# Four-image vision tower on one core: the last image's turn in another order, the block list in five steps, and the expert weights fetched expert by expert into the keys' tile

## The chip, the core and the metric

The program runs on one core of a Trainium2 chip. The metric is the device time of one execution in microseconds. Before the change three executions took 757.95, 759.25 and 761.08 us; the median is 759.25 us.

## The reference

Four images of 3 x 224 x 224 are cut into patches of 8 x 8, which makes 784 tokens of 256 channels for each image. A tokenizer is followed by two layers. The part that matters here is layer 0:

```python
h = tok(x)                                        # [4, 3*784, 256]; the three copies of 784 rows are equal
mn = layernorm(layernorm(h)) * gamma + beta
q, k, v = mn @ Wq, mn @ Wk, mn @ Wv               # 8 heads of 32 channels
g = sigmoid(mn @ Wg + bg)
att = einsum('slhc,tlhc->sth', q, k) * scale      # image s against image t, summed over the tokens
att = softmax(att, axis=1)
h = h + (einsum('sth,tlhc->slhc', att, v) * g).reshape(4, -1, 256) @ Wo + bo
x = layernorm(h)
lg = softmax(relu(x @ router_w1 + b1) @ router_w2 + b2)    # 6 experts
top_w, top_i = top_k(lg, 2)
w = softmax(top_w)
y_e = relu(relu(x @ W1[e]) @ W2[e]) @ W3[e]       # each expert, with biases
h = h + w[0] * y_{top_i[0]} + w[1] * y_{top_i[1]}
```

Attention is between images, with one share for each head and pair of images. Each row then goes through two of six experts. Layer 1 (linear attention and a second mixture of experts) follows and isn't touched.

## The kernel before, in words

**Layout.** All is f32. The residual `h` lies in 25 tiles of 128 rows: six for each image, and a last one with the 16 rows left over of each image. Queries, keys, values and gates are kept turned, with channels on the partitions and the image's 784 tokens along the free axis, in two halves `o` of 128 channels. Keys and queries share one tile, `kq` (L767): first the keys `kT` of half 0 (four images), then of half 1, then two slots for the queries of the current and of the next image.

**Layer 0, image by image.** Four functions make up an image `s`: `products` (L815; a multiplication of the image's queries with the keys of image `t`, with a sum along the tokens, on DVE), `shares_before` and `shares_after` (L827, L841; the matmul `pl` with a head mask, then a softmax of 8 numbers for each partition), `gate_mm` and `gate_act` (L799, L808; matmuls `pg`, then a tanh on ACT), and `first_value` and `values` (L856, L865; the weighted sum of the four images' values, then the gate). `attended` (L883) multiplies by `Wo` (`pwo`), adds to `h` on DVE (L897), negates the mean `nm` (L901) and sums squares on ACT (L903). `scales_of`, `shifts_of` and `rows_of_part` (L909, L914, L920) normalise the rows for the experts; `turn_part`, `router`, `router_logits` (L939, L953, L963) turn them and compute the router's logits; `choose` (L975) takes the two best of six on DVE; `count` (L1027) ranks the rows within their experts with matmuls (`pcount`); `send` (L1043) writes the positions, and GpSimd scatters the rows with indirect DMAs (L1059), 12 for an image, into `xrows` in DRAM, sorted by expert.

**Block list.** `early_blocks` (L1109) is a generator of three steps. It counts the rows of each expert so far (`ptotal`, L1079), marks full blocks of 256 rows (`full`, L1114), numbers them (`pplace`, L1087, and a copy, L1089) and writes for the first seven blocks the row offset and the expert's offset into an integer tile `meta` (`pmeta`, L1097; L1101).

**Experts.** For each block, `load` (L1369) reads the row offset into a register of SyncE (SP) and fetches 256 rows (`xb`); `own_weights` (L1391) reads the expert's offset into a register of DVE and copies that expert's 1540 columns out of the tile `ew` (L1396); `turned` (L1398) turns the rows (`ptb`) and copies them on ACT; `hidden` (L1411) runs two layers (`pb`); `rows_back` (L1431) runs the third (`pyb`), adds the bias and stores to `yrows`. A `load` of an early block waits for the scatters of images 0 and 1 alone, any later one for all.

**What sets the order.** PE, ACT and DVE follow the order written by hand inside `tc.manual_schedule`; SP does so where the block names it. The last image's turn starts at L1455: first the remaining `products`, with the gates, `send` of image 1's rows and the block list between them; then the attention's pool is closed (L1477), a new tile `ew` is taken from the pool of `kq` (L1479), and six DMAs of 768 KB on SP fetch the weights of all experts (L1486 to L1491), with four loads of blocks behind them. As `ew` takes the place of `kq`, the six DMAs wait for the last reader of `kq`. Four loads of layer 1's weights stand next on SP. Then come the values of image 3, the rest of image 2's routing, image 3's attention in the parts `ua` (tiles 0 to 3) and `ub` (4 to 6), and, woven in, the first blocks.

Of the kernel before, what the change touches and what calls it, by code (L numbers as in the profile page):

```python
# [21 lines left out]
F32 = mybir.dt.float32  # L22
I32 = mybir.dt.int32
# [4 lines left out]
P = 128  # L28
TT = 128
NI = 4  # L30
# [9 lines left out]
D = 256  # L40
# [9 lines left out]
E0 = 6  # L50
# [7 lines left out]
NEARLY = -(-(2 * 2 * TPI * TT - E0 * (BLK - 1)) // BLK)  # L58
# [4 lines left out]
EW = 6 * D + 4  # L63
# [5 lines left out]
def tile_vit_tower(ctx: ExitStack, tc: tile.TileContext, a: dict, out: bass.AP):  # L69
    nc = tc.nc  # L70
# [694 lines left out]

    keys = layer0.enter_context(tc.tile_pool(name="keys", bufs=1, reuse_waits="tile"))
    kq = keys.tile([P, 2 * TOK + 4 * SEQ], F32, tag="kq", name="kq")  # L767
    kT = kq[:, : 2 * TOK].rearrange("p (c n) -> p c n", c=2)
    qT2 = kq[:, 2 * TOK :].rearrange("p (s c n) -> p s c n", s=2, c=2)
    att = ctx.enter_context(ExitStack())  # L770
# [44 lines left out]
    def products(s, o, ts=range(NI)):  # L815
        if s >= NI:
            return
        if s not in atts:
            atts[s] = small.tile([P, 2, NI], F32, tag="part", name="part")
        for t in ts:  # L820
            prod = attm.tile([P, SEQ], F32, tag="prod", name="prod")
            nc.vector.scalar_tensor_tensor(  # L822
                prod, qTs[s][:, o, :], 1.0, kT[:, o, t * SEQ : (t + 1) * SEQ],
                ALU.mult, ALU.mult, accum_out=atts[s][:, o, t : t + 1],
            )
# [258 lines left out]
    def numbered(these):  # L1084

        pp = psum_s.tile([P, 512], F32, tag="pss", name="pplace")[:NQ, :1]
        nc.tensor.matmul(pp, before[:NQ, :NQ], these, start=True, stop=True)  # L1087
        place = small.tile([NQ, 1], F32, tag="place", name="place", bufs=1)
        nc.vector.tensor_copy(place, pp)  # L1089
        return place  # L1090

    def meta_of(these, place, n):
        here = small.tile([NQ, NBLK], F32, tag="here", name="here", bufs=1)[:, :n]
        nc.vector.tensor_scalar(here, blk[:, :n], place, these, ALU.is_equal, ALU.mult)
        pm = psum_s.tile([P, 512], F32, tag="pss", name="pmeta")
        for k in range(3):
            nc.tensor.matmul(  # L1097
                pm[:1, k * n : (k + 1) * n], tcol[:, k + 1 : k + 2], here, start=True, stop=True
            )
        meta = small.tile([1, 3, n], I32, tag=f"meta{n}", name="meta", bufs=1)  # L1100
        nc.vector.tensor_tensor(  # L1101
            meta, pm[:1, : 3 * n].rearrange("r (k i) -> r k i", k=3), shift[:, :, :n], ALU.add
        )
        return meta

    metas = {}
    taken = small.tile([NQ, 1], F32, tag="taken", name="taken", bufs=1)

    def early_blocks():  # L1109

        pn = rows_in_all()
        yield
        full = small.tile([NQ, 1], F32, tag="full", name="full", bufs=1)
        nc.vector.scalar_tensor_tensor(  # L1114
            full, pn, -float(BLK), tcol[:, 0:1], ALU.add, ALU.is_ge
        )
        place = numbered(full)
        yield
        nc.vector.tensor_scalar(taken, place, float(NEARLY), full, ALU.is_lt, ALU.mult)
        metas[0] = meta_of(full, place, NEARLY)  # L1120
        yield

    def flag(name, n=1):
# [151 lines left out]
    )  # L1275
    junk = route.tile([TT, D], F32, tag="junk", name="junk")

    def added_rows(s):

        roots_next()  # L1280
        past = (s - 2, 0, TPI)
        if s > 1:
            products(s, 0, [NI - 1])
            choose(past)
        for k, two in enumerate(halves(range(TPI))):
            if s == 1:
                products(s, 0, (range(2), [2], [3])[k])
            elif k == 2:
                products(s, 1, [0])
            attended(s - 1, two)  # L1290
        if s > 1:
            count(past)
# [36 lines left out]
        if s > 1:  # L1329
            mix3(past)  # L1330

    with tc.manual_schedule(engines=by_hand):
        for o in range(2):
            products(0, o, [NI - 1])
        weights_of_images(0)
        gate_mm(0, 0)
        gate_mm(0, 1)
        gate_act(0, 0)
        first_value(0, 0, 0, SEQ, nc.vector)
        first_value(0, 1, 0, SEQ, nc.scalar)  # L1340
        gate_act(0, 1)
        values(0, 0, 0, SEQ)
        for o in range(2):
            q_mm(1, o)
            q_copy(1, o)
        values(0, 1, 0, SEQ)
        keep_left(0)
        for s in range(1, NI - 1):
            added_rows(s)
            weighed(s)  # L1350
        added_rows(NI - 1)
# [103 lines left out]
    s = NI - 1  # L1455
    past, u, ua, ub = (s - 2, 0, TPI), (s - 1, 0, TPI), (s, 0, GT), (s, GT, TPI + 1 - GT)
    rest = (GN, SEQ - GN)
    with tc.manual_schedule(engines=by_hand):
        products(s, 1, [1])
        scales_of(u)  # L1460
        send(past)
        steps = early_blocks()
        next(steps)
        gate_mm(s, 0)
        shifts_of(u)
        products(s, 1, [2])
        next(steps)
        products(s, 1, [3])
        next(steps)
        gate_act(s, 0)  # L1470
        mx = shares_before(s)
        gate_mm(s, 1)
        for _ in steps:
            pass
        gate_act(s, 1)
        shares_after(s, mx)
    att.close()  # L1477
    work[0] = layer0.enter_context(tc.tile_pool(name="blocks", bufs=2, reuse_waits="tile"))
    ew = keys.tile([P, E0, EW], F32, tag="kq", name="ew")  # L1479
    ewf[0] = ew.rearrange("p e n -> p (e n)")  # L1480
    eb3 = work[0].tile([P, E0 * D], F32, tag="eb3", name="eb3", bufs=1)
    nc.gpsimd.dma_start(
        out=eb3, in_=a["L0_ffn_expert_b3"].rearrange("e n -> (e n)").partition_broadcast(P)
    )
    with tc.manual_schedule(engines=by_hand | {ENG.SP}):
        for i, name in enumerate(("expert_w1", "expert_w2", "expert_w3")):  # L1486
            for c in range(2):
                nc.sync.dma_start(
                    out=ew[:, :, (2 * i + c) * D : (2 * i + c + 1) * D],
                    in_=a[f"L0_ffn_{name}"].rearrange("e (c p) n -> c p e n", p=P)[c],  # L1490
                )  # L1491
        for i in range(4):
            load(i)
        first_value(s, 0, 0, GN, nc.vector)
        first_value(s, 1, 0, GN, nc.scalar)
        rows_of_part(u)
        mix1(past)
        values(s, 0, 0, GN)
        values(s, 1, 0, GN)
        turn_part(u)  # L1500
        mix2(past)
        for o in range(2):
            first_value(s, o, *rest, nc.scalar)
        values(s, 0, *rest, range(1, 3))
        attended(s, [0, 1])
        values(s, 0, *rest, range(3, NI))
        attended(s, [2, 3])
        mix3(past)
        values(s, 1, *rest)
        keep_left(s)  # L1510
        router(u)
        scales_of(ua)
        router_logits(u)
        attended(s, [4, 5])
        shifts_of(ua)
        rows_of_part(ua)
        attended(s, [6])
        for i in (0, 1):
            b = cols[:, rows[f"eb{i + 1}_0"] :][:, : 2 * E0].rearrange("p (e r) -> p e r", r=2)
            nc.vector.tensor_copy(ew[:, :, 6 * D + 2 * i : 6 * D + 2 * i + 2], b)  # L1520
        choose(u)
        turned(0)
        turn_part(ua)
        own_weights(0)
        scales_of(ub)
        count(u)
        hidden(0, 0)
        shifts_of(ub)
        rows_of_part(ub, both=True)
        own_weights(1)  # L1530
        turned(1)
        router(ua)
        send(u)
        hidden(0, 1)
        turn_part(ub, both=True)
        router_logits(ua)
        own_weights(2)
        hidden(1, 0)
        rows_back(0)
        load(4)  # L1540
        choose(ua)
        router(ub)
        turned(2)
        hidden(1, 1)
        count(ua)
        hidden(2, 0)
        send(ua)
        rows_back(1)
        load(5)
        router_logits(ub)  # L1550
        own_weights(3)
        turned(3)
        hidden(2, 1)
        choose(ub)
        hidden(3, 0)
        rows_back(2)
        load(6)
        own_weights(4)
        count(ub)
        turned(4)  # L1560
        hidden(3, 1)
        send(ub)
        hidden(4, 0)
        rows_back(3)
        own_weights(5)
        turned(5)
        steps = later_blocks()
        hidden(4, 1)
        next(steps)
        hidden(5, 0)  # L1570
        next(steps)
        rows_back(4)
        next(steps)
        load(7)
        load(8)
        own_weights(6)
        turned(6)
        hidden(5, 1)
        next(steps)
        hidden(6, 0)  # L1580
        next(steps)
        rows_back(5)
        load(9)
        for v in (u, ua, ub):
            mix1(v)
        hidden(6, 1)
        for v in (u, ua, ub):
            mix2(v)
        for v in (u, ua, ub):
            mix3(v)  # L1590
# [715 lines left out]
```

## Time and profile before

| What | Value |
|---|---|
| profiled execution | 760.57 us |
| its span, first to last instruction | 758.9 us |
| median of three executions | 759.25 us |
| PE (matmul) busy | 698.0 us, 92% |
| DVE busy | 480.9 us, 63% |
| ACT busy | 331.1 us, 44% |
| mean granted TensorE clock | 0.975 |
| last image's turn, 241 to 293 us: PE busy | 40.9 of 52 us, granted clock 0.80 |
| expert blocks, 293 to 408 us: PE busy | 106.6 of 115 us, granted clock 1.00 |

The last two rows are the profile's busy times of stretches of the span. A stretch in which one engine is busy nearly throughout is bound by it; one in which none is holds waits between engines, and then the timeline (each instruction with the idle time before it and what ended that) is the view to read. PE records come in pairs, [...]so `gate_mm`'s four products are eight records. A PE record is longer where the granted clock is half.

### The profile page before, as it was taken

To read this page: it belongs to the slowest core of one execution; us is meant where nothing else is said; L and a number is where in the kernel's file an instruction comes from. 1 tells how busy PE (TensorE), PEld (TensorE's weight loads), DVE (VectorE), ACT (ScalarE), POOL (GpSimd) and SP (SyncE) were. 2 spreads that over 40 slices of the span, in tenths; PEclk is the share of its full clock that TensorE was granted. 3 is DMA by queue.
4 is the path that set the end of the run, shared out by engine and by line. 5 is a ranking of instruction groups with operands and counts; after the bars stand their busy time and mean duration, and the time that the engine had idled before them with its cause. 6 is when DMAs were issued, how large, how long until landed. Compare 5 with 4: busy or idle time off the path is not lost.

```text
span 758.9 us, 10590 instructions
## 1 busy us (share of the span) xinstructions
PE 698.0 (92%) x3391; PEld 478.9 (63%) x3391; DVE 480.9 (63%) x1521; ACT 331.1 (44%) x782; POOL 127.1 (17%) x231
## 2 busy tenths in 40 slices
PE   6798989999996879998899999888999999999996
PEld 4645565666564568887788874557677765555553
DVE  4666786778999654456544767799957464444441
ACT  0554776555865554342222326353546322222231
POOL 5400000000034607600003036752000000000000
PEclk9999999999999879999999999899999999999998
DMA  8399999100011864422334352321000013222333
GB/s 196 89 426 424 425 424 424 48 1 1 0 36 48 275 239 136 157 83 78 91 98 125 98 161 71 88 79 43 1 0 2 4 29 114 93 76 62 125 108 98
DMA packets 56117, 96.24 MB, mean 127 GB/s; under 512 B 6375, under 2 KB 46030, under 8 KB 56062
## 3 DMA queue, kind: packets, MB, share of 16 engines
q1 hardware_dynamic: 49648, 79.38, 29.6%
q0 software_dynamic: 5536, 14.32, 6.2%
q10 hardware_dynamic: 878, 1.86, 1.0%
q8 instruction: 27, 0.44, 0.2%
q14 instruction: 28, 0.23, 0.1%
HBM read 30.45 MB, written 65.09 MB: 126 GB/s over the span
## 4 chain that ended last, share of the span: by engine, by line
PE 69%; DVE 19%; ACT 5%; DMA 3%; issue 2%; SPq 1%; DVEq 1%; ACTq 0%
PE pb L1420 12%; PE pe L289 6%; PE pyb L1438 5%; PE ps L289 4%; PE pqk L1881 4%; PE pkv L289 4%; PE pt L280 4%; PE pw L558 3%; PE pwp L300 3%; PE ps L2256 3%; PE pout L2055 3%; PE pout L2060 3%; DVE oT L868 2%; PE pukx L1980 2%; DMA img<-in_x_dram 2%
## 5 line engine op out<-in xcount | busy, mean ns | idle before, releaser
L1059 POOL DMA_INDIRECT xrows<-xn,pos x50 | 52.6, 1051 | 238.0 <-DVE nm L918 191.9
L1643 POOL DMA_INDIRECT ys<-yrows,pos x50 | 51.7, 1033 | 142.7 <-DMA yrows<-yb 124.3
L1420 PE MATMUL pb<-xTb,own 128*128 128x256 f32 (+1 forms) x240 | 54.5, 371 | 8.1 <-DVE own L1396 5.4
L1426 ACT ACTIVATE hb<-pb,own 128x256 f32<-128x256 f32 (+1 forms) x74 | 33.8, 456 | 57.8 <-PE pb L1420 51.5
L1420 PE MATMUL pb<-hb,own 128*128 128x256 f32 (+1 forms) x240 | 52.1, 359 | 0.6 <-DVE hb L1428 0.6
L1438 PE MATMUL pyb<-own,hb 128*128 128x256 f32 x216 | 51.8, 381 | 0.2 <-ACT hb L1426 0.2
L1420 PEld LDWEIGHTS pb<-xTb,own 128*128 128x128 f32 x240 | 41.7, 195 | 16.1 <-ACT hb L1426 7.6
L1881 PE MATMUL pqk<-Wqkv,lxT 128*128 128x512 f32 x100 | 46.6, 613 | 0.2 <-ACT lxT L89 0.2
L289 PE MATMUL pe<-xT,eW 128*128 128x512 f32 (+1 forms) x112 | 46.0, 553 | 0.0
L1438 PEld LDWEIGHTS pyb<-own,hb 128*128 128x128 f32 x216 | 40.3, 190 | 5.9 <-ACT hb L1426 0.6
L1420 PEld LDWEIGHTS pb<-hb,own 128*128 128x128 f32 x240 | 40.5, 190 | 5.3 <-DVE hb L1428 1.2
L558 PE MATMUL pw<-Wall,pT 128*128 128x512 f32 x96 | 42.6, 593 | 0.0
L1409 ACT COPY xTb<-ptb 128x512 f32<-128x512 f32 (+1 forms) x30 | 16.2, 540 | 56.4 <-PE ptb L1405 56.4
L1444 DVE TENSOR_TENSOR yb<-pyb,eb 128x512 f32<-128x512 f32 (+1 forms) x30 | 19.1, 638 | 33.9 <-PE pyb L1438 33.5
L280 PE MATMUL pt<-ident,xn 128*128 128x128 f32 x200 | 30.4, 282 | 10.2 <-DVE xn L584 6.6
L280 PEld LDWEIGHTS pt<-ident,xn 128*128 128x128 f32 x200 | 23.5, 142 | 25.2 <-ACT y L561 6.0
L1428 DVE TENSOR_SCALAR hb<-pb,own 128x256 f32<-128x256 f32 (+1 forms) x46 | 20.5, 447 | 27.9 <-PE pb L1420 21.2
L822 DVE SCALAR_TENSOR_TENSOR prod<-kq 128x784 f32<-128x784 f32 x32 | 30.4, 970 | 6.1 <-ACT kq L1236 3.4
L289 PEld LDWEIGHTS pe<-xT,eW 128*128 128x128 f32 x112 | 20.2, 190 | 21.6 <-issue 16.5
L1396 DVE COPY own<-ew 128x1540 f32 x30 | 28.9, 965 | 6.8 <-ACT xTb L1409 2.7
L1895 ACT ACTIVATE qk<-qk 128x256 f32<-128x256 f32 x50 | 20.4, 408 | 28.4 <-DVE qk L1887 26.0
L1881 PEld LDWEIGHTS pqk<-Wqkv,lxT 128*128 128x128 f32 x100 | 19.0, 197 | 20.4 <-issue 17.9
(416 smaller groups left out, 1473.4 us busy)
## 6 DMA issues: line engine op xcount, KB each, us to landing
xrows<-nothing SPq DMA_DIRECT2D x22, 896.0 KB
yrows<-nothing SPq DMA_DIRECT2D x22, 896.0 KB
out_dram<-h SPq DMA_DIRECT2D x23, 384.0 KB
xb<-xrows SPq DMA_DIRECT2D x24, 256.0 KB
yrows<-yb SPq DMA_DIRECT2D x24, 256.0 KB
ew<-in_L_ffn_expert_w_dram SPq DMA_DIRECT2D x6, 768.0 KB
wb<-wd SPq DMA_DIRECT2D x16, 128.0 KB
img<-in_x_dram SPq DMA_DIRECT2D x2, 588.0 KB
```

The source lines that it names most:

```text
L280: nc.tensor.transpose(pt[:, j * TT : (j + 1) * TT], xn[:, j, c * P : (c + 1) * P], ident[:TT, :TT])
L289: nc.tensor.matmul(pm[: wcols.stop - wcols.start, :n], w[:, c, wcols], xT(c), start=(c == 0), stop=(c == chunks - 1),)
L300: nc.tensor.matmul(pm[:, i, :], xT(c, t), w[:, c, :], start=(c == 0), stop=(c == chunks - 1))
L558: nc.tensor.matmul(pm, pixels(c, tiles[j]), Wall[:, c, :], start=(c == 0), stop=(c == 1))
L822: nc.vector.scalar_tensor_tensor(prod, qTs[s][:, o, :], 1.0, kT[:, o, t * SEQ : (t + 1) * SEQ], ALU.mult, ALU.mult, accum_out=atts[s][:, o ...
L1059: put = nc.gpsimd.indirect_dma_start(out=xrows[:, :], out_offset=bass.IndirectOffsetOnAxis(ap=pos[:, k, t0 + j : t0 + j + 1], axis=0), in_ ...
L1396: nc.vector.tensor_copy(w, ewf[0][:, bass.ds(off, EW)])
L1420: nc.tensor.matmul(pm, wm[:, c, o * P : (o + 1) * P], src[:, c, :], start=(c == 0), stop=(c == 1),)
L1426: nc.scalar.activation(dst[:, o, :], pm, AF.Relu, bias=b)
L1438: nc.tensor.matmul(pm[:, t, :], src[:, c, t * P : (t + 1) * P], wm[:, c, :], start=(c == 0), stop=(c == 1),)
L1643: got = nc.gpsimd.indirect_dma_start(out=y[:, j, k, :], out_offset=None, in_=yrows[:, :], in_offset=bass.IndirectOffsetOnAxis(ap=pos[:, k, ...
L1881: nc.tensor.matmul(pqk, xTs[u][:, c, cut(j, 1)], Wqkv[:, c, : 2 * D], start=(c == 0), stop=(c == 1),)
```

## The change

Four things change, all around the last image's turn; no arithmetic changes.

- The weights' tile `ew` becomes a view of `kq`, without a new allocation. The six DMAs become 18 of 256 KB, three for each expert, so that each waits only for the readers of the region that it overwrites. Those of experts 0 and 1 are issued after the last product with half 0 of the keys, that of expert 2 after product (half 1, image 1), the rest after product (half 1, image 3).
- The block list has five steps: the matmul and the copy of `numbered`, and the matmuls and the sum of `meta_of`, are apart. All four `gate_mm` products of the image come before it, so that on PE the order is `pcount`, all of `pg`, `ptotal`, `pplace`, `pl`, `pmeta`; product (half 1, image 3) comes ahead of the copy of `pplace` on DVE, and `taken`, `here` and `meta` go between the steps of the softmax and the values. On ACT both gates come ahead of the first value of half 1.
- The four first `load`s come after the values of half 0 in program order; on SP they still follow all weights.
- `router(u)` comes before `attended(s, [0, 1])`; `own_weights(0)` and `own_weights(1)` come ahead of `choose(u)`, the first one ahead of `attended(s, [4, 5])`'s DVE part; `turned(0)` is ahead of `attended(s, [6])`; `hidden(0, 0)` ahead of `turn_part(ua)`; `count(u)` behind `router(ua)`.

```diff
+    ew = kq[:, : E0 * EW].rearrange("p (e n) -> p e n", e=E0)
...
-        place = numbered(full)
+        pp = psum_s.tile([P, 512], F32, tag="pss", name="pplace")[:NQ, :1]
+        nc.tensor.matmul(pp, before[:NQ, :NQ], full, start=True, stop=True)
+        yield
+        place = small.tile([NQ, 1], F32, tag="place", name="place", bufs=1)
+        nc.vector.tensor_copy(place, pp)
         yield
         nc.vector.tensor_scalar(taken, place, float(NEARLY), full, ALU.is_lt, ALU.mult)
-        metas[0] = meta_of(full, place, NEARLY)
+        pm, meta = meta_mm(full, place, NEARLY)
+        yield
+        metas[0] = meta_out(pm, meta, NEARLY)
         yield
...
+    def expert_weights(es):
+        for e in es:
+            for i, name in enumerate(("expert_w1", "expert_w2", "expert_w3")):
+                nc.sync.dma_start(
+                    out=ew[:, e, 2 * i * D : 2 * (i + 1) * D].rearrange("p (c n) -> p c n", c=2),
+                    in_=a[f"L0_ffn_{name}"][e].rearrange("(c p) n -> p c n", p=P),
+                )
...
             products(s, 0, [NI - 1])
+            if s == NI - 1:
+                expert_weights(range(2))
             choose(past)
...
-    with tc.manual_schedule(engines=by_hand):
+    with tc.manual_schedule(engines=by_hand | {ENG.SP}):
+        gate_mm(s, 0)
+        gate_mm(s, 1)
         products(s, 1, [1])
+        expert_weights([2])
         scales_of(u)
         send(past)
         steps = early_blocks()
         next(steps)
-        gate_mm(s, 0)
         shifts_of(u)
         products(s, 1, [2])
         next(steps)
+        gate_act(s, 0)
         products(s, 1, [3])
+        expert_weights(range(3, E0))
         next(steps)
-        gate_act(s, 0)
         mx = shares_before(s)
-        gate_mm(s, 1)
-        for _ in steps:
-            pass
+        next(steps)
         gate_act(s, 1)
         shares_after(s, mx)
     att.close()
...
-    ew = keys.tile([P, E0, EW], F32, tag="kq", name="ew")
-    ewf[0] = ew.rearrange("p e n -> p (e n)")
+    ewf[0] = kq[:, : E0 * EW]
...
-        for i, name in enumerate(("expert_w1", "expert_w2", "expert_w3")):
-            for c in range(2):
-                nc.sync.dma_start(
-                    out=ew[:, :, (2 * i + c) * D : (2 * i + c + 1) * D],
-                    in_=a[f"L0_ffn_{name}"].rearrange("e (c p) n -> c p e n", p=P)[c],
-                )
-        for i in range(4):
-            load(i)
...
         values(s, 0, 0, GN)
+        for _ in steps:
+            pass
+        for i in range(4):
+            load(i)
         values(s, 1, 0, GN)
...
             first_value(s, o, *rest, nc.scalar)
+        router(u)
         values(s, 0, *rest, range(1, 3))
         attended(s, [0, 1])
         values(s, 0, *rest, range(3, NI))
         attended(s, [2, 3])
         mix3(past)
+        scales_of(ua)
         values(s, 1, *rest)
         keep_left(s)
-        router(u)
-        scales_of(ua)
         router_logits(u)
-        attended(s, [4, 5])
         shifts_of(ua)
-        rows_of_part(ua)
-        attended(s, [6])
...
+        own_weights(0)
+        attended(s, [4, 5])
+        rows_of_part(ua)
+        turned(0)
+        attended(s, [6])
+        hidden(0, 0)
+        turn_part(ua)
+        own_weights(1)
+        scales_of(ub)
         choose(u)
-        turned(0)
-        turn_part(ua)
-        own_weights(0)
-        scales_of(ub)
-        count(u)
-        hidden(0, 0)
+        turned(1)
         shifts_of(ub)
         rows_of_part(ub, both=True)
-        own_weights(1)
-        turned(1)
         router(ua)
+        count(u)
         send(u)
```

More of the change, by code (lines that the diff above doesn't have):

```diff
@@ L1090, in numbered, with meta_mm @@
         return place
-    def meta_of(these, place, n):
+    def meta_mm(these, place, n):
         here = small.tile([NQ, NBLK], F32, tag="here", name="here", bufs=1)[:, :n]
@@ L1099, in meta_of, with meta_out @@
             )
-        meta = small.tile([1, 3, n], I32, tag=f"meta{n}", name="meta", bufs=1)
+        return pm, small.tile([1, 3, n], I32, tag=f"meta{n}", name="meta", bufs=1)
+    def meta_out(pm, meta, n):
         nc.vector.tensor_tensor(
@@ L1104, in meta_of @@
         return meta
+    def meta_of(these, place, n):
+        return meta_out(*meta_mm(these, place, n), n)
     metas = {}
@@ L1457, in tile_vit_tower @@
     rest = (GN, SEQ - GN)
-    with tc.manual_schedule(engines=by_hand):
+    with tc.manual_schedule(engines=by_hand | {ENG.SP}):
+        gate_mm(s, 0)
+        gate_mm(s, 1)
         products(s, 1, [1])
+        expert_weights([2])
         scales_of(u)
```

## The prediction

> **What bounds the kernel now.** I read the slices first, then busy times by stretch, then the timeline of the weak stretch, then SP's waits.
>
> ```profile
> PE   6798989999996879998899999888999999999996
> ...
> PEclk9999999999999879999999999899999999999998
> DMA  8399999100011864422334352321000013222333
> ```
>
> PE is nearly full everywhere except at the start and in slices 13 to 15 (digits 6, 8, 7; a slice is 19 us), where the clock also drops and the DMA engines are busy. That is the last image's turn.
>
> ```profile
> 200.00:241.00 41.00, 36.08 (x164) 25.65 (x162) 37.96 (x117) 26.47 (x60) 13.68 (x12) 1.00 0.11 39
> 241.00:293.00 52.00, 40.91 (x161) 29.38 (x162) 29.78 (x106) 28.92 (x70) 19.53 (x20) 0.80 0.59 203
> 293.00:408.00 115.00, 106.61 (x591) 91.74 (x590) 60.48 (x154) 37.02 (x84) 20.27 (x25) 1.00 0.33 106
> ```
>
> Columns: length, busy PE, PE's weight loads, DVE, ACT, GpSimd, granted clock, DMA share, GB/s. From 241 to 293 us no engine is full: PE shows 40.9 of 52 us, part of it at half clock, DVE 29.8, ACT 28.9. So waits between engines bound this stretch; before it DVE is full, after it PE.
>
> ```profile
> 244.95 5.25 PE L289 MATMUL pg<-mT,Wg 128*128 128x392 f32 x8
> 250.31 0.15 DVE L1089 COPY place<-pplace 78x1 f32<-78x1 f32 x1 [3.69 <-PE pplace L1087]
> 250.39 0.96 DVE L822 SCALAR_TENSOR_TENSOR prod<-kq 128x784 f32<-128x784 f32 x1
> 251.42 9.86 SPq L1488 DMA_DIRECT2D ew<-in_L_ffn_expert_w_dram  x6
> 252.56 4.57 PE L289 MATMUL pg<-mT,Wg 128*128 128x392 f32 x8
> 257.65 2.55 ACT L933 ACTIVATE xn<-h,nm,r 128x256 f32<-128x256 f32 x5
> 268.65 0.18 DVE L881 COPY oL<-oT 128x32 f32<-128x32 f32 x1
> 273.57 0.51 ACT L903 ACTIVATE junk<-h,nm 128x256 f32<-128x256 f32 x1 [3.53 <-DVE nm L901]
> 279.48 0.96 DVE L1396 COPY own<-ew 128x1540 f32 x1 [1.13 <-DMA bqkv<-in_L_attn_b_qkv_dram]
> 280.59 3.59 PE L1420 MATMUL pb<-xTb,own 128*128 128x256 f32 x8 [1.48 <-DVE r L917]
> ```
>
> The chain to see: PE stands idle from 240.86 (end of `pcount`) to 244.7, its clock falls, and eight gate records take 5.25 us instead of 2.88 (the same eight at 214.17). `pplace` stands behind them on PE, so DVE waits 3.69 us, and the last product, `pl`, the shares, the second gate and ACT's rows are all late. The first block's `pb` then starts only at 280.59.
>
> ```profile
> SPq L1488 <- DVE prod L822: 129.3, 1, 129.3
> SPq L1375 <- DMA xrows<-xn,pos: 2.9, 1, 2.9
> ```
>
> The weights wait for the last product, and the first block load for the scatters.
>
> [...]the clock is 0.50 in 244.7 to 246 and 0.57 in 270 to 274, and gate records take 0.65 us there against 0.36. [...]a scatter lands after 5.5 us (median) in 240 to 285 us, against 2.5 in 200 to 240. [...]here `own` starts 1.13 us after its predecessor the first time, 0.39 the second, so I take 1.13 and keep 0.39 as the other end.
>
> **The change, part by part** (times of the old run, then of mine).
>
> *Gates first.* All sixteen records follow `pcount` at 240.86 with PE warm: 16 x 0.36 = 5.8, to 246.6. `ptotal` 0.4, then `full` 0.15, which DVE reaches at 246.5, so it waits 0.5; behind it stands the last product, behind that `pl` and the last weights. The product ends at 248.2 (old 251.4). `pl` and the softmax take 1.7 as before, plus 0.2 for `taken` and `here` put between: shares at 250.05 (old 253.95). Gain 3.9.
>
> *ACT.* Both gates are ready, so after the exponential: 2 x 0.53, first value 0.72, six rows x 0.52: 254.2 (old 260.2). Gain 6.0; the old order waited 1.0 for the second gate.
>
> *Values.* DVE's 6.63 us from first value to gated half 1, plus 0.2 for `meta`: 256.9; 0.7 for `mix2`: 257.55. Transposes end at about 255.4, since the clock will be at half from about 250 (PE has little to do from 247 to 252). `router(u)` (2.74 us at full clock) comes first now, loses some 0.7 at half clock, and ends at 258.7. `pwo` for tiles 0 and 1: 8 x 0.22, ready at 260.45. DVE waits there about 1.1 us; from this wait's end to `oL` the old run took 268.83 - 263.42 = 5.4, so `oL` is done at 265.85. Gain shrinks to 3.0: `router(u)` ahead of `pwo` eats the rest.
>
> *Block 0.* `pwo` for 4 and 5 starts at 266.1, mostly at half clock: 268.8; `ptb` 0.6; `pwo` for 6, 1.7: 271.1. DVE: shifts and bias copies 0.9, then `own(0)` 1.13 + 0.96, to 268.85; so it fits under `pwo`. If PE were quicker, it would cost up to 1.3, for `h`, squares and rows stand behind it. `h` 0.9 to 269.8; ACT: two squares 1.14, four rows 2.06, `xTb` 0.56: 273.6. `pb` starts at 273.65 (old 280.59). Gain 6.9: `choose(u)` (3.6) and two waits are no longer ahead of it.
>
> *Given back.* Old: 8.9 us from the end of that `pb` to the end of `pyb`. Now eight transposes and `ptb` come after it, and `router(ua)` waits for ACT's two `hb` and two `xT` copies (1.5 us instead of 0.45 after `pb`), and `pcount(u)` (0.5) stands in the row: 10.5. `pb` 273.65 + 3.59 + 10.5 = 287.7 against 293.1: 5.4.
>
> *Weights and loads.* 18 issues at 0.46 (the row of the 256 KB `Wout`) are 8.3 us of SP, not more than the old 9.86, and behind them stand only loads that wait for scatters. The 4.7 MB at some 390 GB/s need 12 us: experts 0 and 1 from 235.7, 2 from 243.5, the rest 6 us from 248.2, all in by 256, 11 us before `own(0)`. So the early fetch itself is worth nothing on the path; it lets `own(0)` move and frees the DMA engines: GpSimd's twelve scatters still end at 260.65, but land at about 262, and loads start at 262.3 instead of 266.24. `ptb` needs its rows at 268.8; without that relief rows would come around 269, a cost of some 0.5. The four loads of layer 1's weights behind them move too, with nobody waiting.
>
> *After 288.* The order per engine in the built program is the old one from there on, and PE is full (106.6 of 115 us), so the gain passes. GpSimd's last 26 scatters run back to back from 284.34; now `send(u)` gives positions at about 281.7, so they end only 2 us earlier. Block 7's load needs them: landed at about 319, loaded at 321, used about 329. Slack 8; it doesn't decide.
>
> *Sum.* 5.4, less 0.4[...]: 5.0. The profiled execution is 760.57 (span 758.9 and 1.7 around it), and would become 755.6; it stands 1.3 above the median, so I take the gain from the median: 759.25 - 5.0 = 754.2.
>
> **Rivals.** *Small gain, 757.0.* `router(u)` at half clock throughout (1.9 more than at full, 1.2 more than mine) and half clock again in block 0's last products, 1.6: the gain is 2.2. For it: PE has a thin load between 247 and 255. Against: transposes alone kept the clock up in 257 to 260.
>
> *Large gain, 750.7.* The clock stays up in `pwo` (1.2) and `pb` (1.6), and the register load takes 0.4 instead of 1.13: 3.5 more. For it: PE's gaps are shorter than before. Against: `plg` and a gap of 2.5 us precede `pwo`, as they preceded the fall at 270.
>
> *Slower, 764.* One mechanism: [...]after the gates it gets only short bursts behind ACT and DVE. Then about 10 us more lie on the path: `router` and `pwo` 5, block 0 and `router(ua)` 5. 754.2 + 10 = 764. It decides once 5 us are lost[...].
>
> That the fetch doesn't start early is no rival of weight: if it waited as before, weights would be in by about 260, still ahead of `own(0)`.
>
> **How the numbers follow.** Forecast 0.50, small gain 0.22, large gain 0.17, slower 0.11. Faster or slower by 0.5% (3.8 us) is about what a measurement of this kernel can tell from no change. Forecast counts as faster except for 0.04; large gain is faster; small gain is within, but for 0.02; of the slower case 0.02 stay within. Faster 0.65, same 0.25, slower 0.10. The range runs from 749.5, beyond the large gain by the spread of the old runs, to 758.5, beyond the small gain by the same; only the slower case and tails lie outside.
>
> **What would show it.** Sixteen `pg` records of 0.36 us in a row up to 246.6; the last product ending near 248; no DVE wait of 3.7 us on `pplace`; weights' issues from 235.7; first load near 262; rows of image 2 ending near 254; `oL` near 266; first `pb` near 273.7, first `pyb` ending near 288. If `oL` isn't earlier by 2 us or more, or PE shows half clock after 284, I am wrong; if blocks after 293 no longer start one behind another, scatters or loads became the bound.

## The result, and the profile after

| | before | after |
|---|---|---|
| median of five executions | 761.0 us (757.95 to 762.25) | 754.54 us (753.87 to 755.8) |
| profiled execution, its span | 760.57, 758.9 us | 754.25, 752.5 us |

The ratio is 0.9925 (95% interval 0.99 to 0.995). 754.2 us was forecast. The gain of the medians is 6.5 us where 5.0 was forecast, but two more executions of the kernel before have moved its median from 759.25 to 761.0. In the experiments, executions of one kernel spread by 1 to 3%, and the ratios given there leave out those over 1.5% above the fastest, so they are read beside the medians of all executions.

The slices of the changed kernel:

```profile
PE   7898989999998869997899999879999999999996
...
PEclk9899999999999889999999999998999999999999
DMA  8399999100014754432324352331000013322333
```

The weak place at slices 13 to 15 is still there, a little shallower; the DMA share now rises in slice 13 already (digit 4 instead of 1), since the first weights are issued from 223.1 us on. The same stretches as before, up to the first block's end (288 us instead of 293):

```profile
241.00:288.00 47.00, 36.79 (x163) 27.39 (x163) 30.04 (x108) 29.14 (x72) 16.99 (x17) 0.85 0.55 182
288.00:403.00 115.00, 106.27 (x590) 91.47 (x589) 60.05 (x154) 37.03 (x84) 23.38 (x28) 1.00 0.34 109
```

The last image's turn takes 47 us instead of 52, with the same work: DVE 30.0 and ACT 29.1 us as before, PE 36.8 instead of 40.9 at a mean clock of 0.85 instead of 0.80. The block stage behind it is unchanged. The timeline of that stretch, in the order of the forecast's steps:

```profile
241.09 5.51 PE L289 MATMUL pg<-mT,Wg 128*128 128x392 f32 x16
247.82 0.15 DVE L1127 COPY place<-pplace 78x1 f32<-78x1 f32 x1
249.69 0.49 DVE L864 TENSOR_SCALAR oT<-vT,att 128x512 f32<-128x512 f32 x1
254.62 4.25 PE L289 MATMUL pr<-xT,rw 128*128 128x512 f32 x8
260.63 0.42 DVE L898 SCALAR_TENSOR_TENSOR h<-pwo,h 128x256 f32<-128x256 f32 x1 [2.00 <-PE pwo L300]
265.87 0.18 DVE L882 COPY oL<-oT 128x32 f32<-128x32 f32 x1
265.89 1.56 PE L300 MATMUL pwo<-Wo,oT 128*128 128x256 f32 x6 [1.80 <-DVE oT L874]
267.99 0.96 DVE L1418 COPY own<-kq 128x1540 f32 x1 [1.11 <-DMA xb<-xrows]
268.87 0.42 DVE L898 SCALAR_TENSOR_TENSOR h<-pwo,h 128x256 f32<-128x256 f32 x1
272.99 0.56 ACT L1431 COPY xTb<-ptb 128x512 f32<-128x512 f32 x1
273.60 3.78 PE L1442 MATMUL pb<-xTb,own 128*128 128x256 f32 x8 [4.85 <-ACT xTb L1431]
288.33 0.69 DVE L1466 TENSOR_TENSOR yb<-pyb,eb 128x512 f32<-128x512 f32 x1 [2.62 <-PE pyb L1460]
```

To see: the gates run in one piece; the copy of `pplace`, which ended a wait of 3.69 us before, shows no wait; the first `pb` starts 7.0 us earlier, though it now waits 4.85 us for `xTb`; the first `yb` comes at 288.33 instead of 293.10.

```profile
SPq L1293 <- DVE prod L823: 115.1, 5, 98.7
SPq L1397 <- DMA xrows<-xn,pos: 10.3, 2, 8.4
```

In SP's waits the weights now wait for single products. Four of the 18 are issued from 223.1 us and two more at 236.2, where the forecast had 235.7 for the first. The first load waits 8.4 us for the scatters instead of 2.9: it is ready early, and the scatters, not the weights, set when it goes.

### The profile page after: what moved, and what is told of

It is laid out like the page before. It is cut to its first block, busy times and chain, and to the rows that moved or that the text cites. A ratio compares the mean times of both kernels' runs of the same rounds, so it can differ in the third digit from the quotient of the medians.

```text
span 752.5 us, 10617 instructions
## 1 busy us (share of the span) xinstructions
PE 695.0 (92%) x3391; PEld 480.3 (64%) x3391; DVE 480.1 (64%) x1521; ACT 330.9 (44%) x782; POOL 126.7 (17%) x231
## 4 chain that ended last, share of the span: by engine, by line
PE 54%; DVE 6%; ACT 1%; issue 1%; DMA 1%; DVEq 0%; SPq 0%; ACTq 0%
PE pb L1442 12%; PE pe L289 6%; PE pyb L1460 5%; PE ps L289 4%; PE pqk L1899 4%; PE ps L2274 3%; PE pout L2073 3%; PE pout L2078 3%; PE pt L280 3%; PE pukx L1998 2%; PE pe L2244 2%; PE ps L2268 2%; PE ptb L1427 1%; DVE h L1675 1%; PE pkvo L2058 1%
## 5 line engine op out<-in xcount | busy, mean ns | idle before, releaser
L1899 PE MATMUL pqk<-Wqkv,lxT 128*128 128x512 f32 x100 | 45.0, 595 | 0.2 <-ACT lxT L89 0.2
L1450 DVE TENSOR_SCALAR hb<-pb,own 128x256 f32<-128x256 f32 (+1 forms) x46 | 20.5, 446 | 27.9 <-PE pb L1442 21.2
L1418 DVE COPY own<-kq 128x1540 f32 x30 | 28.8, 963 | 7.4 <-ACT xTb L1431 2.7
```

What stands on the lines that cost most here:

```text
L1418: nc.vector.tensor_copy(w, ewf[0][:, bass.ds(off, EW)])
L1899: nc.tensor.matmul(pqk, xTs[u][:, c, cut(j, 1)], Wqkv[:, c, : 2 * D], start=(c == 0), stop=(c == 1),)
```

## The experiments

They ran on chips on which the kernel before takes 781 us instead of 761 (780.93 to 781.87, medians of 50 to 67 executions for each set of four runs). Both kernels have been run there too. Two stretches are read in each trace: from the end of the last `pcount` near 241 us to the end of PE's records of the first `pyb` (nearly all that the change moves), and from there to the start of the fourth `yb`. The expectations speak of the first `yb` instead of the end of `pyb`. In most runs it follows 0.04 us later, but in g1 and e4 DVE stood 5.0 and 4.0 us between the two without a reason on record, so the first `yb` isn't a fair end there.

| run | median, us (executions) | ratio to before (95%) | `pcount` to end of first `pyb` | from there to fourth `yb` |
|---|---|---|---|---|
| first pair, before | 761.0 (5) | | 52.20 | 20.53 |
| first pair, after | 754.54 (5) | 0.9925 (0.99 to 0.995) | 47.04 | 20.52 |
| e1_late_fetch | 778.65 (12) | 1.0005 (0.9965 to 1.0045) | 50.02 | 29.95 |
| e2_gates_first_only | 780.17 (20) | 1.0031 (0.9996 to 1.0066) | 52.09 | 26.60 |
| e3_later_order_only | 787.9 (20) | 1.007 (1.0031 to 1.0108) | 54.71 | 34.21 |
| e4_fetch_only | 782.31 (20) | 1.0034 (1.0003 to 1.0066) | 52.89 | 28.67 |
| f1_fetch_at_end | 778.62 (14) | 0.9996 (0.9961 to 1.003) | 50.14 | 29.07 |
| f2_choose_first | 782.86 (22) | 1.0008 (0.9974 to 1.0042) | 53.56 | 29.95 |
| f3_turn_first | 775.17 (22) | 0.9929 (0.9896 to 0.9962) | 45.24 | 29.89 |
| f4_filled_gap | 778.74 (22) | 1.0057 (1.0021 to 1.0092) | 47.70 | 34.11 |
| g1_before_again | 782.75 (14) | 1.0029 (0.9991 to 1.0066) | 52.97 | 31.06 |
| g2_changed_again | 777.42 (22) | 0.9985 (0.9958 to 1.0012) | 49.74 | 29.95 |
| g3_turn_first_again | 773.42 (12) | 0.9938 (0.99 to 0.9976) | 45.31 | 29.70 |
| g4_own_early | 774.05 (15) | 0.9911 (0.9882 to 0.9939) | 45.45 | 29.91 |

### Both kernels on one chip, and a stop behind the first block

g1 and g2 are the two kernels, unchanged.

> The kernel before, unchanged, so that its profile comes from the same chip as those of the other runs of this set. All eight runs so far lie near 780 us, where the first pair had 761 and 754.5, and in seven of their eight profiles DVE and ACT stand 6 to 9 us between 290 and 310 us, before `at` of image 3's rows or the copies around it, with no releaser that the profile knows. Theory A (the stop belongs to these chips): the kernel before shows it too, its first and fourth yb lie 25 to 34 us apart instead of 20.5, and the stretch from the end of pcount (241) to the first yb is 52 to 57 us. Theory B (the stop came with the change, which gives its gain back there): first to fourth yb 20 to 22 us. If this chip shows no stop in any of the four, the first pair's numbers come again: 761 us.

> The changed kernel, unchanged. By my theory of the change the stretch from the end of pcount to the first yb is 4 to 6.5 us shorter than that of the kernel before on the same chip, and the median 3 to 6.5 us below. Rival (the gain is lost behind the first yb): the stretch is shorter by as much, but the median differs by less than 1.5 us, and what was gained is gone by the fourth yb.

Up to the first `yb` the stretch is 8.2 us shorter (57.94 to 49.78), more than the 4 to 6.5 expected. But 5.0 us of that are a stop of DVE in g1, behind the work that the change moves:

```profile
293.66 1.89 PE L1438 MATMUL pyb<-own,hb 128*128 128x256 f32 x8
300.52 0.69 DVE L1444 TENSOR_TENSOR yb<-pyb,eb 128x512 f32<-128x512 f32 x1 [7.47 <-PE pb L1420]
```

`pyb` is over at 295.55, and `yb` starts at 300.52. Up to the end of `pyb` the changed kernel is 3.2 us shorter (52.97 to 49.74), less than expected, and from there to the fourth `yb` both kernels take about the same, 31.1 and 30.0 us, where the first pair had 20.5 in both. The medians of all executions differ by 3.5 us (780.93 to 777.42; by 5.3 against g1's own executions), in the expected range. The ratio's interval still reaches 1.0012, so this set alone doesn't show a gain. The waits of DVE, then of ACT, from 283 us on in g2:

```profile
DVE at L1049 <- remote: 8.1, 1, 8.1
```

```profile
ACT hb L1448 <- remote: 5.3, 1, 5.3
```

"Remote" means that no recorded event explains the release. The same view of ACT in g1:

```profile
ACT hb L1426 <- remote: 6.5, 2, 4.1
```

So theory A holds: the kernel before has the stop too, and loses as much by it. Theory B isn't borne out; in g1 the stop only begins earlier, ahead of the first `yb`. Its cause is open. One observation: for the eight semaphores on which GpSimd's DMAs land, nearly all of them scatters and gathers, the first pair's traces record 1888 and 1887 landings, the twelve others 722 to 847. The missing ones lie from 220 to 340 and from 400 to 540 us, and the stops lie in these stretches too. A wait is called "remote" because its release wasn't recorded, so the name and the missing records may say the same thing twice; that the engines stand longer is in the times themselves. No run took the scatters away, and what stops the engines stays untested.

### Which part brings the gain

e1 was meant to issue all weights after the last product; e2 and e3 were to take the first half's new order alone and the second's alone, both with that late fetch; e4 is the old order with the early fetch.

```diff
-            if s == NI - 1:
-                expert_weights(range(2))
...
-        expert_weights([2])
...
-        expert_weights(range(3, E0))
+        expert_weights(range(E0))
```

> The changed kernel with all 18 weight DMAs behind the last product (half 1, image 3); every other order as changed. Theory (the two reorderings give the gain, the early fetch only frees the DMA engines): last product still ends near 248, weights land near 261, the first block load is issued 1 to 3 us later than 263.0, first pb later by 0 to 1.5 us; time 0 to 1.5 us above the changed kernel's, so 754.5 to 756. Rival (the fetch gives the gain): back to 758 or more, with pb waiting for own's weights.

> The gates and the block list in the new order, weights fetched behind the last product, and everything from router(u) on in the old order. Theory: rows of image 2 end near 253.5 as in the changed kernel, oL 4 to 5 us earlier than 268.7, first pyb ends 3 to 4.5 us earlier than 293.1; gain 3 to 4.5 us, so it is the larger part. Rival (the gain is the later order, with own and choose): gain under 2 us.

> The gates and the block list in the old order, weights behind the last product, and from router(u) on the new order. Theory: router(u) ahead of pwo delays oL by some 1.6 us, own ahead of choose wins 4, given back 1.6: gain 0.5 to 1.5 us by the first pyb, within noise in the time. Rival (the later order gives the gain): gain of 3 us or more, first pb at 276 or earlier.

> The kernel before with the weights fetched in 18 DMAs as regions of the keys come free; every order on PE, DVE and ACT as before. Theory: block loads move from 266.2 to 262 to 263, nothing on PE moves, first pb within 0.5 us of 280.6, time within 0.5 us of before. Rival (the fetch gives the gain): 4 us or more faster.

e1 missed its aim. In e1 the weight DMAs waited for the readers of their regions of `kq`, not for their place in the program: nothing else stood before them on SP, so the first weights were still issued from 221.3 us, and every engine had the changed kernel's order. e1 is therefore one more execution of the changed kernel (50.02 us up to the end of `pyb`, g2 49.74), and e2 and e3 had the early fetch as well.

Early fetch alone (e4) is worth 0.1 us: 52.89 against g1's 52.97, with the first block load issued 21.2 instead of 25.3 us after `pcount`. Gates first and the list in five steps (e2) bring the shares 3.3 us earlier than in e4 (8.3 instead of 11.5 us after `pcount`), and `oL` as much. At the end of `pyb` 0.8 us are left (52.09), as DVE then waits longer for `pwo`, first e2, then e4:

```profile
272.85 0.42 DVE L898 SCALAR_TENSOR_TENSOR h<-pwo,h 128x256 f32<-128x256 f32 x1 [4.33 <-PE pwo L300]
273.98 0.42 DVE L898 SCALAR_TENSOR_TENSOR h<-pwo,h 128x256 f32<-128x256 f32 x1 [2.65 <-PE pwo L300]
```

The later order alone (e3) is 1.8 us longer than e4 (54.71). Both together are 2.9 (e1) to 3.2 us (g2) shorter. So e2 fell short of its 3 to 4.5 us and e3 of its 0.5 to 1.5, and in these traces neither reordering brings the gain without the other.

How the gain divides isn't settled by that. e3's profiled execution took 792.92 us, 5 us above the median of its own executions. And on these chips the kernels with the old first half (g1, e4, e3) have a wait without a reason on record inside the stretch, before ACT's last gate: 3.1 to 3.6 us where the first pair's old kernel waits 1.0 for PE's `pg`. In e4 that `pg` had ended at 254.61:

```profile
258.87 0.59 ACT L812 ACTIVATE gate<-pg,bgh 128x392 f32<-128x392 f32 x1 [3.10 <-issue]
```

The medians don't divide it either (e3 is slowest of all), since behind the first `pyb` each version has its own stop, 26.6 to 34.2 us up to the fourth `yb`.

### A fetch that is really late

f1 is the changed kernel, but `ew` is again a new tile of the keys' pool.

```diff
-    ew = kq[:, : E0 * EW].rearrange("p (e n) -> p e n", e=E0)
...
-    ewf[0] = kq[:, : E0 * EW]
+    ew = keys.tile([P, E0, EW], F32, tag="kq", name="ew")
+    ewf[0] = ew.rearrange("p e n -> p (e n)")
...
+        expert_weights(range(E0))
         first_value(s, 0, 0, GN, nc.vector)
```

> The changed kernel, but the weights go into a tile that is taken anew from the keys' pool, so that all 18 fetches wait for the last reader of the keys (last product, near 248 us) and then stand on SP ahead of the block loads. Orders on PE, DVE and ACT are those of the changed kernel. My theory (the early fetch is worth at most 0.5 us on the path): weights' issues from 248 to 257, weights in by 263, scatters land later, first block load issued near 266 instead of 263, its rows in near 269; ptb and the last pwo slip by 1 to 2 us, but the first pb still waits for xTb behind ACT's rows, so it starts within 0.5 us of 273.6 and the time is 754.5 to 755.5 where the changed kernel takes 754.5. Rival (the new order needs the early fetch): own(0) or ptb waits for its data past 271, the first pb starts at 276 or later, time 757 to 759.

The weights are issued from 250.5 us, just behind the last product, and the first load goes at 268.1, 24.2 us after `pcount` instead of 21.8 in g2. On PE:

```profile
273.76 1.09 PE L1424 MATMUL ptb<-ident,xb 128*128 128x128 f32 x4 [1.36 <-DMA xb<-xrows]
274.64 1.91 PE L300 MATMUL pwo<-Wo,oL 128*128 128x256 f32 x4
278.80 3.78 PE L1439 MATMUL pb<-xTb,own 128*128 128x256 f32 x8 [2.24 <-ACT xTb L1428]
```

`ptb` does wait 1.36 us for its rows, but `pb` still waits for `xTb` behind ACT's rows. The stretch is 50.14 us against 49.74 and 50.02, the median 778.62 against 778.65 and 777.42. The early fetch is worth nothing that this can tell, also in the new order.

### The order of choose, own and h

f2 puts `choose(u)` ahead of `own_weights(0)` again.

```diff
+        choose(u)
         own_weights(0)
...
         scales_of(ub)
-        choose(u)
         turned(1)
```

> The changed kernel, but choose(u) stands ahead of own_weights(0) again, as before the change. My theory (on DVE the order of choose, own and h decides when the first pb starts): 18 small DVE instructions, 4.6 us from the first lg to the last tiles, go ahead of own(0) and of h for tiles 4 and 5; h, the squares, the rows and xTb behind it slip by some 4.4 us, the first pb starts near 278 instead of 273.6, some of it is regained since the choice is ready long before pcount: first yb 3 to 4.4 us later than 288.3, time 757.5 to 759. Rival (the time is set by PE's clock and by router(ua), not by DVE's order): first yb within 1 us, time 754 to 755.5.

```profile
280.54 3.78 PE L1442 MATMUL pb<-xTb,own 128*128 128x256 f32 x8 [6.84 <-ACT xTb L1431]
```

The first `pb` starts 38.4 us after `pcount` instead of 34.7 (g2), 3.7 us later; the stretch is 3.8 us longer than g2's and the median is 782.86 against 777.42 to 778.65. As expected: DVE's order counts, as ACT's squares and rows, and behind them `xTb`, wait for `h`.

### The wait of 4.85 us for xTb

f3 and g3 are one kernel: `turned(0)` goes ahead of `attended(s, [4, 5])`. g4 also moves the bias copies and `own_weights(0)` ahead of `attended(s, [0, 1])`.

```diff
         own_weights(0)
+        turned(0)
         attended(s, [4, 5])
         rows_of_part(ua)
-        turned(0)
```

> The changed kernel, but turned(0) (ptb on PE and the copy xTb on ACT) stands ahead of attended(s,[4,5]) instead of behind the rows of ua. My theory (the first pb waits 4.85 us for xTb only because ACT has two squares and four rows ahead of it): xTb is copied near 266.5 to 268 in a gap of ACT, the first pb starts near 269.1, when own(0) is done, and is over before the rows of ua are; their transposes then start near 273.2 instead of 277.2, though at half clock; first yb 1.5 to 3 us earlier than 288.3, time 751.5 to 753. Rival (what follows pb is bound by ACT, by hb and xT, or by the clock, and not by pb): first yb within 0.7 us, time 754 to 755. Third: ptb waits for the rows of block 0 past 266 and holds up pwo for tiles 4 and 5 by over 1 us: slower, 755.5 to 757.

> The version with turned(0) ahead of attended(s,[4,5]) again, beside the changed kernel on one chip. My theory: the first pb starts when own(0) and the last pwo are done instead of behind ACT's rows, 2.5 to 4.5 us earlier in the count from pcount's end; first yb 2 to 5 us earlier; median 2 to 4.5 us below that of the changed kernel. Rival (its lead over the changed kernel in the last set was the chip's, since the changed kernel had not run there): median within 1 us.

> As the version before it, and the bias copies and own_weights(0) stand ahead of attended(s,[0,1]) on DVE, where the changed kernel waited 2.0 us for pwo; possible only with the weights fetched early, by 258 us. My theory: bias copies, register load and copy (0.24 + 1.1 + 0.96 us) fill that wait and cost 0.3 to 0.5 us there; behind oL the 2.3 us are gone, h for tiles 4 and 5 waits for pwo alone, and rows and the transposes of ua start 0.5 to 1.5 us earlier; median 0.3 to 1.5 us below that of the version before it. Rival (the weights are not in by 258.6): DVE waits for them, h for tiles 0 and 1 is late by over 1 us, and the median is 0.5 to 2 us above. Second rival (pwo for tiles 4 and 5 runs at half clock and ends as late as own(0) did): no difference, within 0.5 us.

PE in g3:

```profile
266.36 3.07 PE L300 MATMUL pwo<-Wo,oT 128*128 128x256 f32 x8
269.27 1.03 PE L300 MATMUL pwo<-Wo,oL 128*128 128x256 f32 x4
270.13 1.89 PE L1442 MATMUL pb<-xTb,own 128*128 128x256 f32 x8
272.61 0.33 PE L280 MATMUL pt<-ident,xn 128*128 128x128 f32 x1 [0.59 <-ACT xn L934]
```

`pb` follows `pwo` without a wait, 30.3 us after `pcount` instead of 34.7, and at full clock: 1.89 us instead of 3.78. It ends before ACT's rows are there. The end of `pyb` is 4.4 us earlier than in g2, the median 4.0 us lower (773.42 against 777.42; in the other set 775.17). f3's own expectation, 1.5 to 3 us, was too low: it had PE at half clock behind `pb`, and in g3 the half clock was over before `pb` began (3.07 us for the eight `pwo` records before it, 1.89 us for `pb`). This version beats both kernels: 0.9938 of the kernel before (0.99 to 0.9976), where the changed kernel has 0.9985 (0.9958 to 1.0012).

g4 adds nothing (774.05 against 773.42; stretch 45.45 against 45.31). Its second rival is what happened. DVE in g4:

```profile
260.98 0.96 DVE L1418 COPY own<-kq 128x1540 f32 x1 [0.78 <-issue]
272.32 0.42 DVE L898 SCALAR_TENSOR_TENSOR h<-pwo,h 128x256 f32<-128x256 f32 x1 [2.29 <-PE pwo L300]
```

The copy fits, with the weights there by 261 us, but the 2.3 us it leaves turn into a wait for `pwo`, which is at half clock there (3.00 us for its eight records).

### The clock in the gap

f4 fills PE's idle stretch before the first `pb` with products that nobody reads.

```diff
         attended(s, [6])
+        fill = ps_tile("fill")
+        for _ in range(5):
+            nc.tensor.matmul(fill, ident, h[:, 0:2, :], start=True, stop=True)
         hidden(0, 0)
```

> The changed kernel with five added matmuls of 512 columns (ten records of about 0.48 us) into a PSUM tile that nobody reads, on PE between the last pwo (268.7) and the first pb (273.6). My theory (the half clock from 270 to 277 comes from PE's idle stretch before it, and costs the first pb 1.9 us and the transposes behind it 0.4): the clock stays up, the fill ends near 273.5, the first pb takes 1.9 us instead of 3.78, first yb some 2 us earlier than 288.3, time 752 to 753. Rival (the clock falls at 270 anyway, because of what lies before 268.7): the fill runs at half clock and ends near 277, the first pb starts over 3 us late, time 757 to 758.

```profile
273.08 4.45 PE L1543 MATMUL fill<-h,ident 128*128 128x512 f32 x10
277.37 1.89 PE L1442 MATMUL pb<-xTb,own 128*128 128x256 f32 x8
```

The clock holds: `pb` takes 1.89 us, where g2's takes 3.78 us behind an idle gap of 3.47 us, and `pyb` ends 2.0 us earlier than in g2. So the half clock on the first `pb` does come from the gap before it. But the stretch with the stop behind the first block is 4.2 us longer (34.11 against 29.95), and the median, 778.74, shows no gain.

## Why the prediction was right

The mechanism was right: on the first pair's traces the steps agree in place and size. How the gain divides among them was not shown (e2 to e4).

- **Gates first.** Sixteen records to 246.6 us, as forecast; the product ended at 247.9 (forecast 248.2), the shares were there at 249.7 (250.05). e2 has this step too, but its gain was nearly used up before the end of `pyb`, and it was expected to keep 3 us or more.
- **Router ahead of `pwo`.** Forecast end 258.7; PE went on to `pwo` at 258.70. DVE waited 2.00 us for `pwo` instead of 1.1, because its values had ended at 256.3 and not 256.9, and `pwo` was ready 0.2 us later; `oL` was done at 266.05 (265.85).
- **Block 0.** `pb` started at 273.60 (273.65), and yet one term was wrong: "`pwo` for 4 and 5 starts at 266.1, mostly at half clock: 268.8". It ran at full clock (1.56 us for six records, 2.93 in g2 at half clock), though `plg` and a wait of 1.80 us stood ahead of it, where the old run's fall at 270 had `plg` and a wait of 1.27; PE was through with `pwo` at 268.8 instead of 271.1. That brought nothing, and the next sentences of the prediction say why: if PE were quicker, `own(0)` would cost up to 1.3 us, as `h` stands behind it. `h` started at 268.87, 1.4 us after its product was ready. So the error stayed hidden, since `own(0)` had been forecast to end at the same time as `pwo`. That is luck: with `own(0)` elsewhere the term would have counted. On the later chips `pwo` is at half clock (3.07 us for eight records in g3), and g4 shows the other side: without `own(0)` there, DVE waits for `pwo`.
- **Given back.** From the end of `pb` to the end of `pyb` 10.9 us (10.5 forecast, 8.9 before).
- **The early fetch worth nothing on the path.** f1 and e4 (0.1 us) confirm it. Its start was wrong, 223.1 us instead of 235.7: the forecast went by the place in the program.
- **After 288.** Not foreseen in part. By the spans: the changed stretch gives 5.2 us (5.4 forecast). The changed kernel's `pcount` ended 0.4 us later, with nothing of the change before it but the first six weight DMAs, and the blocks lose another 0.3. Layer 1, where nothing is changed, gains 1.8 us: the last `yb` to the first `kn` is 31.83 instead of 32.59, the rest 268.89 instead of 269.93. Half clock in other places would fit (10.2 us of it in both kernels, in 485.2 to 492.1 and 515.9 to 519.4 us before, in 479.5 to 483.0 and 506.8 to 513.7 after), but that is argued and not shown.

So the total was met by a stretch that is well forecast, and by a remainder of 1.1 us that nobody forecast and which another execution may not repeat. That the time was met within 0.4 us is luck in part: the median of the kernel before rose by 1.75 us, and the larger gain made up for it. The slower rival, half clock all through 250 to 284 us, didn't come: the clock was half in 250.8 to 257.6 and 271.3 to 278.1 us, 6.8 us each and 13.7 in all. In the old run it was half for 20.5 us in this turn, in four stretches of 6.8, 3.4, 3.4 and 6.8 us. PE wasn't wholly idle before a fall: it was busy for 0.7 us from 247.4 to 250.8 and for 0.9 us from 267.9 to 271.3. Which idle time makes the clock fall, and for how long, was the author's estimate; these runs don't show a rule for it.

## What to carry over

Where several engines wait for each other, write down for each instruction that starts a chain what else is late at that moment: taking away one cover (`pwo` at half clock) or moving one cost (`own(0)`) changed nothing alone, because the other stood right behind it. In the same way the new order of the gates gave 3.3 us at `oL` and 0.8 us at the end of `pyb`. A wait that a change leaves behind, like the 4.85 us for `xTb`, names the next edit: a copy with its inputs ready that is queued behind work with a later input on the same engine should go ahead of it (4.4 us at the end of `pyb` in g3). And moving the weight DMAs in the program didn't move them in time, as their only wait was on a region of `kq` (221.3 us in e1, 223.1 in the first pair); made to wait for the last reader of the whole tile, they came at 250.5 us (f1). And a stretch should end at an event that what follows can't move: with the first `yb` as the end, a stop of DVE that belongs to the next stretch counted as a gain of 5 us.

## What the runs showed of the hardware

- Missing records and stops went together, with the cause open: with 1887 or 1888 landings recorded, no wait marked "remote" on PE, DVE or ACT; with 722 to 847, stops of DVE and ACT, the longest where GpSimd's scatters run beside the blocks (DVE 8.1 us at 303 us in g2) and near 500 us, where its gathers run (ACT 8.5 us at 498 us in g3), and 20 us more in all.
- A filled gap kept the clock up: with ten records of no use (4.45 us) before it in f4, the same `pb` took 1.89 us instead of the 3.78 of g2 and of the first pair.
- Ahead of the copy `own(0)` DVE stands 1.11 us in the first pair's changed kernel, ahead of the next one 0.63. The register load itself took 0.55 and 0.32 us there, the register arithmetic behind it 0.25 and 0.24 us; ahead of `own(0)` four semaphore records of at most 0.05 us followed, from 267.6 to 267.9 us.
